# GpSimd's large operations in the recurrent layers: one a step, issued between VectorE's two products, and r projected before v

## The chip, the cores and the metric

One core of a Trainium2 chip runs the whole program. The metric is the device time of one execution in microseconds; smaller is better. Five engines work side by side, each in the order its instructions were issued: TensorE (PE in the profile, with PEld for its weight loads), VectorE (DVE), ScalarE (ACT), GpSimd (POOL) and SyncE (SP, which issues weight loads). Work on one engine waits for another through semaphores.

## The reference, cut to what matters

Four layers run one after the other on x (4 x 512 x 512, float32) and a context of the same shape: a cross attention (layer 0), two recurrent layers (1 and 2), and a perceiver attention with an MLP (layer 3). The change is in the recurrent layers. One of them computes, for a batch element and 512 time steps, with 32 heads of 16:

```
xa = layer_norm(x);  sx = previous_row(xa) - xa                 # "shift"
t  = tanh((xa + sx * maa_x) @ maa_w1)                            # first mix
m_j = t_j @ maa_w2_j;  x_j = xa + sx * (maa_j + m_j)             # j in w, k, v, r, g
w = exp(-exp(decay + tanh(xw @ dw1) @ dw2))
r, k, v = xr @ Wr, xk @ Wk, xv @ Wv;   g = silu(xg @ Wg)
for each step l:  a = k_l (x) v_l                                # outer product per head
    out_l = r_l . (faaaa * a + s);   s = a + w_l * s
y = group_norm(out) * gn_w + gn_b
x = x + (y * g) @ Wo
xc = layer_norm(x);  sxc = previous_row(xc) - xc                 # "shift" again
x = x + sigmoid((xc + sxc*fr) @ fWr) * (relu((xc + sxc*fk) @ fWk)**2 @ fWv)
```

The term faaaa * a needs only r*k summed over a head, times v: in the kernel ruk (faaaa * r * k), al (its sum by a matmul) and y = v * al.

## The kernel before, in words

`recurrent` cuts the two layers into 16 units (2 layers, 4 batch elements, 2 halves of TS = 256 rows), and each unit into G = 8 steps of the recurrence. A step g is: `begun(g+1)` multiplies the repeated v (in PSUM) with k (in SBUF) twice on VectorE, into kv and into A (line 833), copies the state into kv's first column (839), lets GpSimd add A onto kv by an accumulating DMA (`added`, 584), and has ScalarE copy the decay into W (844). `scan(g)` runs VectorE's scan over W and kv (866) and then two products with r, called ry (871). `summed(g-1)` sums an earlier step's ry on TensorE into py (885). A has one buffer, so the A product of a step waits until the DMA of the step before has landed. kv has two buffers.

Around the steps stand three generators for every unit: `mixes` (norm, shift, the five mixes, the projections), `outputs` (group norm, gate, Wo) and `channels` (the second half of the layer). Each yields a step and a phase (EARLY, SOON, MID, LATE) at which its next piece is issued. Steps count from the unit's own first step, so in any step pieces of several units meet: `mixes` of the next unit at -11 to 0, `outputs` of the last one at 9 to 15, `channels` of the one before it at 19 to 27. In the text "step 7" means any step with that place in a unit. The order inside a step is written out by hand: summed, begun, scan, the repetition of v (814) in every fourth, then the phases. The planner takes this order as it is; engines run ahead of one another only as far as buffers allow. PSUM has three rotating banks for all projections (`pp`), one for py and a single buffer for the repeated v.

GpSimd has six large operations a unit, each over 128 partitions: the shift of the mixes, sx (588, 128x1020, with a small second part for the first column, 589); ruk times k (772); v times al into y (799); the addition of rk onto half of y (800); y's gate, yg times g (958); and the shift of the channels, sxc (588, 589). In the kernel before they are issued in the phases, where their data come to be ready: sx at -9 MID, ruk at -2 EARLY, both y at 0 LATE, yg at 14 EARLY, sxc at 22 MID. Other work on GpSimd's queue: all accumulating DMAs (kv, mixes, xk, xr, x), and two small powers of 6.5 us for the group norm (933, 935).

ScalarE evacuates the projections: o_v, o_k, o_r (702) with two scalings ruk after each half of r (705), the gate o_g (698, finished by VectorE's `gated`, 717), the mixes (665), xk and xr from sxc (996), rp from the group norm's power (939), the gated output's scaling yg (951). The gate o_g has two buffers; one is read until yg's multiplication is over.

TensorE's order in the steps at which the change bites: step 7 is xa's transposes (ptn), Wo, then the next step's py; step 0 is al, the first mix (mixx with w1, two groups), xk's projection fk, and the first pair of mixes (w and k); step 1 is py, the mean, the second pair (v and r) and xr's projection pr; step 2 is py, the repetition vr, var; step 4 is v's projection, step 5 pbc and r's, step 6 py, vr, transposes, g's.

Of the kernel before, what the change touches and what calls it, by code (L numbers as in the profile page):

```python
# [8 lines left out]
F32 = mybir.dt.float32  # L9
I32 = mybir.dt.int32  # L10
AF = mybir.ActivationFunctionType
ALU = mybir.AluOpType
# [3 lines left out]
P = 128  # L16
# [5 lines left out]
BUFS = {"mix": 4, "cx": 3}  # L22
# [8 lines left out]
def tile_xattn_rwkv_perceiver(ctx: ExitStack, tc: tile.TileContext, t: dict, out: bass.AP):  # L31
    nc = tc.nc
# [422 lines left out]
    def recurrent(lp, ep, beside):  # L455
# [4 lines left out]
        G = 2 * NI  # L460
        TP = TS // 2
        EARLY, SOON, MID, LATE = range(4)

        mp = sp = mq = sq = pvr = pyp = W = A = None
# [19 lines left out]
        gmean = lp.tile([P, P], F32, name="gmean")  # L484
        nc.vector.tensor_scalar(gmean, gself, 1.0 / HS, None, ALU.mult)

        rp = lp.tile([P, TS], F32, name="rp")
        nc.gpsimd.memset(rp, 0.0)
        stT = lp.tile([P, KC, B, 2], F32, name="stT")
# [50 lines left out]
        def seconds(a):  # L540
            return a[:, :, TP:]
# [44 lines left out]
        def shift(sx, cur, before):  # L586

            nc.gpsimd.tensor_tensor(sx[:, :, 1:], cur[:, :, : TS - 1], cur[:, :, 1:], ALU.subtract)
            nc.gpsimd.tensor_tensor(sx[:, :, 0], before, cur[:, :, 0], ALU.subtract)

        st = {}

        def mixes(q):

# [20 lines left out]
            else:  # L615
                both = wpool.tile([P, 2, KC, TS], F32, tag="w", name="sx0")
                sx, mix = both[:, 0], both[:, 1]
            shift(sx, cur, stT[:, :, b, 1] if hf == 0 else st[q - 1]["last"])
            yield (-10, EARLY) if q == 1 else (-9, LATE)
            if mp:  # L620
                mix = mp.tile([P, KC, TS], F32, tag="mix", name="mixx", bufs=BUFS["mix"])
            for k in range(KC):
                nc.vector.scalar_tensor_tensor(
                    mix[:, k], sx[:, k], vec[:, k, V_MAAX : V_MAAX + 1], cur[:, k], ALU.mult, ALU.add
                )
            yield (-10, MID) if q == 1 else (-8, EARLY)
            th = lp.tile([P, 2, TS], F32, tag="th", name="th")
            pm = psum_tile([P, TS], "pm")
            mm(pm, [(c["w1"][:, k, :P], mix[:, k, :]) for k in range(KC)])
# [86 lines left out]
                for dst, pm in gates:  # L716
                    nc.vector.scalar_tensor_tensor(dst, dst, 1.0, pm, ALU.add, ALU.mult)

            yield (-7, EARLY) if q == 1 else (-8, LATE)
            second("wk")  # L720
            yield -7, MID if q == 1 else EARLY
            second("vr")
            yield -7, LATE
            mixed("wk")
# [28 lines left out]
            yield -5, LATE  # L753
            second("g")
            yield -4, MID
            if q > 0:
                product("v")
            else:
                ruk = mp.tile(full, F32, tag="mix", name="ruk", bufs=BUFS["mix"])
                product("r")  # L760
            yield -4, LATE
            mixed("g")
            yield -3, MID
            if q > 0:
                ruk = mp.tile(full, F32, tag="mix", name="ruk", bufs=BUFS["mix"])
                product("r")
            else:
                product("v")
                repeated(0, 0)
            yield -2, EARLY  # L770
            k, r = d["k"], d["r"]
            nc.gpsimd.tensor_tensor(ruk, ruk, k, ALU.mult)
            rk = mp.tile([P, NI, TP], F32, tag="rk", name="rk", bufs=1)
            nc.vector.tensor_tensor(rk, seconds(r), firsts(k), ALU.mult)
            D = d["D"] = mp.tile([P, NI, TP], F32, tag="D", name="D", bufs=1)
# [20 lines left out]
            )  # L796
            yield 0, LATE
            y = d["y"] = mq.tile(full, F32, tag="y", name="y")
            nc.gpsimd.tensor_tensor(y, d["v"], al[:, None, :].to_broadcast(full), ALU.mult)
            nc.gpsimd.tensor_tensor(seconds(y), seconds(y), rk, ALU.add)  # L800
            if q == 0:
                product("g")
                yield 1, LATE
# [21 lines left out]
        def begun(g):  # L825

            q, e, i = place(g)
            d = st[q]
            if units[q][2]:
                d["S"] = st[q - 1]["S"]  # L830
            kv = kvs[g] = mp.tile([P, 8, TP + 1], F32, tag="kv", name="kv")
            for half, dst in ((seconds, kv), (firsts, A)):
                nc.vector.tensor_tensor(
                    dst[:, :, 1:],
                    half(vrs[q, e].rearrange("p q f l -> p (q f) l")),
                    half(d["k"][:, i : i + 1, :]).to_broadcast([P, 8, TP]),
                    ALU.mult,
                )
            nc.vector.tensor_copy(quarters(kv)[:, :, :, 0], states(q)[:, i, e])  # L839
            if g == 0:  # L840
                nc.vector.tensor_tensor(flat(kv), flat(kv), flat(A), ALU.add)
            else:
                added(flat(kv), flat(A))
            nc.scalar.copy(W[g % 2][:, :, 1:], d["D"][:, i : i + 1, :].to_broadcast([P, 8, TP]))
# [5 lines left out]
        def quarters(kv):  # L850
            return kv.rearrange("p (q f) l -> p q f l", f=2)

        def states(q):
            return st[q]["S"].rearrange("p i (q e f) -> p i e q f", e=2, f=2)
# [45 lines left out]
        def outputs(q):  # L900
# [41 lines left out]
            mm(pm, [(gself, rp)])  # L942
            bc = sq.tile([P, TS], F32, tag="mean", name="bc", bufs=1)
            nc.scalar.copy(bc, pm)
            yield 13, LATE
            nc.vector.tensor_tensor(y, y, bc[:, None, :].to_broadcast(full), ALU.mult)
            yield 14, EARLY

            yg = mq.tile(full, F32, tag="cx", name="yg", bufs=BUFS["cx"])
            for i in range(NI):  # L950
# [4 lines left out]
                    bias=c["gn"][:, i, 1:2],  # L955
                    scale=c["gn"][:, i, 0:1],
                )
            nc.gpsimd.tensor_tensor(yg, yg, d["g"], ALU.mult)
            yield 15, MID
            wo = wpool.tile([P, NI, C], F32, tag="w", name=n + "wo")  # L960
            for a in range(4):
# [13 lines left out]
        def channels(q):  # L975
# [12 lines left out]
            nc.scalar.copy(last, cur[:, :, TS - 1])  # L988
            yield 22, MID
            sx = mq.tile([P, KC, TS], F32, tag="sxc", name="sxc", bufs=1)  # L990
            shift(sx, cur, stT[:, :, b, 0] if hf == 0 else st[q - 1]["lastc"])

            def shifted(name, i):
                dst = mq.tile([P, KC, TS], F32, tag="cx", name=name, bufs=BUFS["cx"])
# [2 lines left out]
                added(dst, cur)  # L997
                return dst

            yield 23, EARLY  # L1000
            xk = shifted("xk", V_FK)
            yield 23, LATE
            xr = shifted("xr", V_FR)
# [59 lines left out]
        with ExitStack() as below, ExitStack() as above:  # L1063
            mq = below.enter_context(tc.tile_pool(name="rq", bufs=2))
            sq = below.enter_context(tc.tile_pool(name="rt2", bufs=2))
            pp = below.enter_context(tc.tile_pool(name="rpp", bufs=3, space=PSUM))
            mp = above.enter_context(tc.tile_pool(name="rm", bufs=2))
            sp = above.enter_context(tc.tile_pool(name="rs", bufs=2))
            pvr = above.enter_context(tc.tile_pool(name="rpv", bufs=1, space=PSUM))
            pyp = above.enter_context(tc.tile_pool(name="rpy", bufs=1, space=PSUM))  # L1070
            psum["p"] = pp, "p"


            W = [mp.tile([P, 8, TP + 1], F32, tag=f"W{i}", name=f"W{i}", bufs=1) for i in range(2)]
            A = mp.tile([P, 8, TP + 1], F32, tag="A", name="A", bufs=1)
            for z in (*W, A):
                nc.gpsimd.memset(z[:, :, 0:1], 0.0)
            for g in range(at[0], end + 28):
                if 0 < g <= end:
                    summed(g - 1)  # L1080
                if -1 <= g < end - 1:
                    begun(g + 1)
                if 0 <= g < end:
                    scan(g)
                if 0 < g < end - 2 and g % NI == NI - 2:
                    repeated(*place(g + 2)[:2])
                for ph in (EARLY, SOON, MID, LATE):
                    for q, gen in steps.pop((g, ph), ()):
                        at = next(gen, None)
                        if at:  # L1090
                            follow(q, at, gen)
                    if ph == MID and 0 < g <= end and g % NI == 0:
                        taken(g - 1)
                if g == end:
                    above.close()
                elif g > end:
                    next(beside, None)
            for _ in beside:
                pass
# [409 lines left out]
```

## Time and profile before

| what | value |
|---|---|
| median of 3 runs | 3722.05 us (3721.71 to 3724.03) |
| span of the profiled execution | 3715.9 us |
| the profiled execution's own time | not given apart from its span; the runs lie 5.8 to 8.1 us above it |
| TensorE, VectorE, ScalarE, GpSimd busy | 95%, 73%, 45%, 47% of the span |
| recurrent steps (first scan to the end of the last py) | about 781 to 2254 us |
| layer 3 alone | from about 2410 us |
| ry (871) | 256 of 1598 ns in the mean, 398.6 us |
| scan (866) | 128 of 2311 ns, 295.9 us |

A row of a group or timeline gives the line, the engine, the operation, the output and its inputs by the program's names, the shape, how often, and the busy time; in brackets stand the engine's idle time before it and what ended it. A busy TensorE is not TensorE at its peak, since ends of pipelined matmuls are modelled. In a table of windows the columns are the length, the busy time (and number) for PE, PEld, DVE, ACT and POOL, the granted TensorE clock, the share of the DMA engines and GB/s.

### The profile page before, as it was taken

The numbers are of one execution on the slowest core, as the hardware profiler recorded it, in microseconds if no ns is written. First come the engines' busy times: TensorE is split into PE (matmuls) and PEld (weight loads), VectorE is DVE, ScalarE is ACT, GpSimd is POOL, SyncE is SP. The second block draws the span as 40 slices with busy tenths as digits, with TensorE's granted clock in tenths as the row PEclk, the third lists the DMA queues.
The fourth block names the chain that finished last, engine by engine and source line by source line (L and its number), as shares of the span: only waits on it lengthen the run. The fifth ranks groups of instructions, "written<-read, shape, count | busy, mean of one in ns | idle before, by whom it ended". The sixth has DMA issues, their size and how long they took to land. (4 is left out here: it accounts for less than half of the span.)

```text
span 3715.9 us, 52436 instructions
## 1 busy us (share of the span) xinstructions
PE 3545.8 (95%) x20544; PEld 1885.9 (51%) x20544; DVE 2728.7 (73%) x4601; ACT 1675.7 (45%) x2550; POOL 1743.4 (47%) x850
## 2 busy tenths in 40 slices
PE   8999999998899999999999988999999999999989
PEld 3333333365566665666666644444455444544446
DVE  6777777679988888888888883388855676667531
ACT  4777676544444444444444433233344334434421
POOL 4777777524444444444444443065533343444430
PEclk9999999999999999999999998999999999999999
DMA  4000000056677777777777775300022212121223
GB/s 154 24 12 24 12 9 21 24 130 140 146 177 175 177 187 182 176 175 177 177 175 177 177 167 134 102 26 18 23 88 77 72 52 88 60 71 35 97 97 125
DMA packets 188806, 386.67 MB, mean 104 GB/s; under 512 B 18128, under 2 KB 44880, under 8 KB 186512
## 3 DMA queue, kind: packets, MB, share of 16 engines
q1 hardware_dynamic: 150256, 251.72, 21.2%
q0 software_dynamic: 38304, 131.61, 19.4%
q8 instruction: 162, 2.65, 0.3%
q14 instruction: 84, 0.69, 0.1%
HBM read 247.50 MB, written 4.19 MB: 68 GB/s over the span
## 5 line engine op out<-in xcount | busy, mean ns | idle before, releaser
L1253 POOL TENSOR_TENSOR acc<-acc,aT 128x2048 f32<-128x2048 f32 x96 | 436.2, 4544 | 336.2 <-ACT aT L1248 219.6
L292 POOL TENSOR_TENSOR aT<-aT,nmT 128x1536 f32<-128x1536 f32 x124 | 428.6, 3460 | 206.1 <-ACT aT L290 182.8
L254 DVE CUSTOM_DVE_ANT_0 sc<-psc,nm 128x512 f32<-128x512 f32 x512 | 353.8, 691 | 146.8 <-PE psc L242 89.1
L1237 DVE TENSOR_TENSOR aT<-pst,mb 128x512 f32<-128x512 f32 x512 | 317.5, 681 | 163.2 <-PE pst L1192 163.2
L871 DVE TENSOR_TENSOR ry<-kv,o_r 128x1024 f32<-128x1024 f32 x256 | 398.6, 1598 | 7.2 <-PE pm L73 0.5
L866 DVE TENSOR_TENSOR_SCAN kv<-W,kv 128x1032 f32<-128x1032 f32 x128 | 295.9, 2311 | 0.0
L584 POOL DMA_DIRECT2D kv<-A x127 | 111.4, 877 | 358.0 <-DVE kv L839 220.0
L290 ACT COPY aT<-pst 128x512 f32<-128x512 f32 x372 | 196.5, 594 | 177.2 <-PE pst L279 176.8
L298 ACT ACTIVATE aT<-aT 128x2048 f32<-128x2048 f32 x128 | 246.7, 1929 | 5.5 <-POOL aT L292 4.8
L73 PE MATMUL ph<-nT,l_m 128*128 128x256 f32 x1024 | 235.9, 385 | 0.0
L73 PE MATMUL po<-l_m,hT 128*128 128x512 f32 x512 | 233.1, 601 | 0.0
L73 PEld LDWEIGHTS ph<-nT,l_m 128*128 128x128 f32 x1024 | 191.8, 191 | 64.2 <-issue 24.8
L1206 DVE CUSTOM_DVE_ANT_0 sc<-psc,zeros,mx 128x512 f32<-128x512 f32 x256 | 176.6, 745 | 56.2 <-PE psc L1192 47.1
L279 PE MATMUL pst<-q,km 32*128 32x512 f32 x1024 | 206.3, 639 | 9.4 <-DVE mxs L254 5.8
L1248 ACT ACTIVATE aT<-aT 128x2048 f32<-128x2048 f32 x64 | 122.3, 1910 | 190.6 <-DVE aT L1237 185.7
L1246 ACT ACTIVATE aT<-aT,mc 128x2048 f32<-128x2048 f32 x64 | 128.1, 2002 | 162.6 <-DVE aT L1237 156.3
L1206 DVE CUSTOM_DVE_ANT_0 sc<-psc,nm 128x512 f32<-128x512 f32 x256 | 161.1, 684 | 52.2 <-PE psc L1192 52.2
L242 PE MATMUL psc<-km,q 32*128 32x512 f32 x1024 | 197.8, 650 | 0.8 <-ACT q L223 0.8
L885 PE MATMUL py<-ry,k 128*32 128x512 f32 x1024 | 161.9, 625 | 38.3 <-DVE ry L871 25.6
L1192 PE MATMUL pst<-q,kT 32*128 32x512 f32 x1024 | 183.1, 649 | 0.0
L1192 PE MATMUL psc<-kT,q 32*128 32x512 f32 x1024 | 171.0, 644 | 12.3 <-DVE aT L1237 11.5
L1251 POOL TENSOR_TENSOR acc<-aT 128x2048 f32<-128x2048 f32 x16 | 72.5, 4532 | 234.2 <-ACT aT L1246 234.2
(266 smaller groups left out, 6999.6 us busy)
## 6 DMA issues: line engine op xcount, KB each, us to landing
l_m<-in_L_W SPq DMA_DIRECT2D x64, 1024.0 KB, 5.1
kv<-A POOLq DMA_DIRECT2D x127, 516.0 KB, 6.1
L_wk<-in_L_Wk SPq DMA_DIRECT2D x16, 1024.0 KB, 8.0
L_wr<-in_L_Wr SPq DMA_DIRECT2D x16, 1024.0 KB, 7.2
L_wv<-in_L_Wv SPq DMA_DIRECT2D x16, 1024.0 KB, 5.8
L_wg<-in_L_Wg SPq DMA_DIRECT2D x16, 1024.0 KB, 7.6
L_wo<-in_L_Wo SPq DMA_DIRECT2D x64, 256.0 KB, 4.9
L_fk<-in_L_fWk SPq DMA_DIRECT2D x16, 1024.0 KB, 6.8
```

The lines of the kernel that those rows point to most:

```text
L73: nc.tensor.matmul(ps, lhsT, rhs, start=(i == 0), stop=(i == len(pairs) - 1))
L242: nc.tensor.matmul(psc, d["q"][g][rs, lt * P : (lt + 1) * P], d["km"][rs, a, :], start=True, stop=True, tile_position=(32 * r, 0),)
L254: nc.vector.tensor_tensor_reduce(sc, ps[r], d["nm"][lt], 1.0, -3.0e38, ALU.add, ALU.max, mxs[:, a, lt, c : c + 1])
L279: nc.tensor.matmul(pst, d["km"][rs, a, s * P : (s + 1) * P], d["q2", a][rs, :], start=True, stop=True, tile_position=(32 * r, 0),)
L292: nc.gpsimd.tensor_tensor(w[:, n:, :], w[:, n:, :], nmT[:, None, :].to_broadcast([P, NR - n, L]), ALU.add)
L298: nc.scalar.activation(w, w, AF.Exp)
L866: nc.vector.tensor_tensor_scan(flat(kv), flat(W[g % 2]), flat(kv), 0.0, ALU.mult, ALU.add)
L871: nc.vector.tensor_tensor(y, kv[:, 4 * h : 4 * h + 4, None, :TP].to_broadcast([P, 4, 2, TP]), d["r"][:, i].rearrange("p (o m) -> p o m", o ...
L1192: nc.tensor.matmul(psc, lhsT[rs], rhs[rs], start=True, stop=True, tile_position=(32 * r, 0))
L1206: nc.vector.tensor_tensor_reduce(sc, ps[r], d["nm"][a], 1.0, mx[:, 0, lt, r : r + 1] if a else 3.0e38, ALU.add, ALU.min, mx[:, a, lt, r : ...
L1237: nc.vector.tensor_tensor(w[:, r, :], ps[r], d["mb"][:, r, :], ALU.subtract)
L1253: nc.gpsimd.tensor_tensor(d["acc", m], d["acc", m], w, ALU.add)
```

## The change

A helper `pooled` collects the six large operations in `slots`, by step. `begun` issues those of the current step after the kv and A products have been issued, behind a GpSimd copy of one element of kv to a tile `mark`; the copy makes GpSimd wait for the kv product, not for A. The operations are set to steps -8 (sx), -3 (ruk), 1 and 2 (y), 14 (yg) and 23 (sxc), one in any step. kv's DMA is issued on GpSimd's queue after them. For the first two units the steps below 0 are issued at once. The copy of the state moves ahead of the products. r is projected before v in every unit. The first mix moves from -9 LATE and -8 EARLY to -8 EARLY and -8 LATE, behind fk; the pairs of mixes from -8 LATE and -7 EARLY to -7 EARLY and -7 MID; y times bc from 13 LATE to 13 MID, yg's scaling from 14 EARLY to 13 LATE, and xk from 23 EARLY to 23 SOON.

```diff
--- before.py
+++ after.py
@@ -484,6 +484,7 @@
         gmean = lp.tile([P, P], F32, name="gmean")
         nc.vector.tensor_scalar(gmean, gself, 1.0 / HS, None, ALU.mult)
 
+        mark = lp.tile([P, 1], F32, name="mark")
         rp = lp.tile([P, TS], F32, name="rp")
         nc.gpsimd.memset(rp, 0.0)
         stT = lp.tile([P, KC, B, 2], F32, name="stT")
@@ -589,6 +590,14 @@
             nc.gpsimd.tensor_tensor(sx[:, :, 0], before, cur[:, :, 0], ALU.subtract)
 
         st = {}
+        slots = {}
+
+        def pooled(q, at, f, *args):
+
+            if q < 2 and at < 0:
+                f(*args)
+            else:
+                slots.setdefault(G * q + at, []).append(lambda: f(*args))
 
         def mixes(q):
 
@@ -615,15 +624,15 @@
             else:
                 both = wpool.tile([P, 2, KC, TS], F32, tag="w", name="sx0")
                 sx, mix = both[:, 0], both[:, 1]
-            shift(sx, cur, stT[:, :, b, 1] if hf == 0 else st[q - 1]["last"])
-            yield (-10, EARLY) if q == 1 else (-9, LATE)
+            pooled(q, -8, shift, sx, cur, stT[:, :, b, 1] if hf == 0 else st[q - 1]["last"])
+            yield (-10, EARLY) if q == 1 else (-8, EARLY)
             if mp:
                 mix = mp.tile([P, KC, TS], F32, tag="mix", name="mixx", bufs=BUFS["mix"])
             for k in range(KC):
                 nc.vector.scalar_tensor_tensor(
                     mix[:, k], sx[:, k], vec[:, k, V_MAAX : V_MAAX + 1], cur[:, k], ALU.mult, ALU.add
                 )
-            yield (-10, MID) if q == 1 else (-8, EARLY)
+            yield (-10, MID) if q == 1 else (-8, LATE)
             th = lp.tile([P, 2, TS], F32, tag="th", name="th")
             pm = psum_tile([P, TS], "pm")
             mm(pm, [(c["w1"][:, k, :P], mix[:, k, :]) for k in range(KC)])
@@ -716,9 +725,9 @@
                 for dst, pm in gates:
                     nc.vector.scalar_tensor_tensor(dst, dst, 1.0, pm, ALU.add, ALU.mult)
 
-            yield (-7, EARLY) if q == 1 else (-8, LATE)
+            yield -7, EARLY
             second("wk")
-            yield -7, MID if q == 1 else EARLY
+            yield -7, MID
             second("vr")
             yield -7, LATE
             mixed("wk")
@@ -753,23 +762,17 @@
             yield -5, LATE
             second("g")
             yield -4, MID
-            if q > 0:
-                product("v")
-            else:
-                ruk = mp.tile(full, F32, tag="mix", name="ruk", bufs=BUFS["mix"])
-                product("r")
+            ruk = mp.tile(full, F32, tag="mix", name="ruk", bufs=BUFS["mix"])
+            product("r")
+            k, r = d["k"], d["r"]
+            pooled(q, -3, nc.gpsimd.tensor_tensor, ruk, ruk, k, ALU.mult)
             yield -4, LATE
             mixed("g")
             yield -3, MID
-            if q > 0:
-                ruk = mp.tile(full, F32, tag="mix", name="ruk", bufs=BUFS["mix"])
-                product("r")
-            else:
-                product("v")
+            product("v")
+            if q == 0:
                 repeated(0, 0)
             yield -2, EARLY
-            k, r = d["k"], d["r"]
-            nc.gpsimd.tensor_tensor(ruk, ruk, k, ALU.mult)
             rk = mp.tile([P, NI, TP], F32, tag="rk", name="rk", bufs=1)
             nc.vector.tensor_tensor(rk, seconds(r), firsts(k), ALU.mult)
             D = d["D"] = mp.tile([P, NI, TP], F32, tag="D", name="D", bufs=1)
@@ -796,8 +799,8 @@
             )
             yield 0, LATE
             y = d["y"] = mq.tile(full, F32, tag="y", name="y")
-            nc.gpsimd.tensor_tensor(y, d["v"], al[:, None, :].to_broadcast(full), ALU.mult)
-            nc.gpsimd.tensor_tensor(seconds(y), seconds(y), rk, ALU.add)
+            pooled(q, 1, nc.gpsimd.tensor_tensor, y, d["v"], al[:, None, :].to_broadcast(full), ALU.mult)
+            pooled(q, 2, nc.gpsimd.tensor_tensor, seconds(y), seconds(y), rk, ALU.add)
             if q == 0:
                 product("g")
                 yield 1, LATE
@@ -829,6 +832,7 @@
             if units[q][2]:
                 d["S"] = st[q - 1]["S"]
             kv = kvs[g] = mp.tile([P, 8, TP + 1], F32, tag="kv", name="kv")
+            nc.vector.tensor_copy(quarters(kv)[:, :, :, 0], states(q)[:, i, e])
             for half, dst in ((seconds, kv), (firsts, A)):
                 nc.vector.tensor_tensor(
                     dst[:, :, 1:],
@@ -836,7 +840,11 @@
                     half(d["k"][:, i : i + 1, :]).to_broadcast([P, 8, TP]),
                     ALU.mult,
                 )
-            nc.vector.tensor_copy(quarters(kv)[:, :, :, 0], states(q)[:, i, e])
+            large = slots.pop(g - 1, ())
+            if large:
+                nc.gpsimd.tensor_copy(mark, kv[:, 0, 1:2])
+            for f in large:
+                f()
             if g == 0:
                 nc.vector.tensor_tensor(flat(kv), flat(kv), flat(A), ALU.add)
             else:
@@ -942,9 +950,9 @@
             mm(pm, [(gself, rp)])
             bc = sq.tile([P, TS], F32, tag="mean", name="bc", bufs=1)
             nc.scalar.copy(bc, pm)
+            yield 13, MID
+            nc.vector.tensor_tensor(y, y, bc[:, None, :].to_broadcast(full), ALU.mult)
             yield 13, LATE
-            nc.vector.tensor_tensor(y, y, bc[:, None, :].to_broadcast(full), ALU.mult)
-            yield 14, EARLY
 
             yg = mq.tile(full, F32, tag="cx", name="yg", bufs=BUFS["cx"])
             for i in range(NI):
@@ -955,7 +963,7 @@
                     bias=c["gn"][:, i, 1:2],
                     scale=c["gn"][:, i, 0:1],
                 )
-            nc.gpsimd.tensor_tensor(yg, yg, d["g"], ALU.mult)
+            pooled(q, 14, nc.gpsimd.tensor_tensor, yg, yg, d["g"], ALU.mult)
             yield 15, MID
             wo = wpool.tile([P, NI, C], F32, tag="w", name=n + "wo")
             for a in range(4):
@@ -988,7 +996,7 @@
             nc.scalar.copy(last, cur[:, :, TS - 1])
             yield 22, MID
             sx = mq.tile([P, KC, TS], F32, tag="sxc", name="sxc", bufs=1)
-            shift(sx, cur, stT[:, :, b, 0] if hf == 0 else st[q - 1]["lastc"])
+            pooled(q, 23, shift, sx, cur, stT[:, :, b, 0] if hf == 0 else st[q - 1]["lastc"])
 
             def shifted(name, i):
                 dst = mq.tile([P, KC, TS], F32, tag="cx", name=name, bufs=BUFS["cx"])
@@ -997,7 +1005,7 @@
                 added(dst, cur)
                 return dst
 
-            yield 23, EARLY
+            yield 23, SOON
             xk = shifted("xk", V_FK)
             yield 23, LATE
             xr = shifted("xr", V_FR)
@@ -1080,6 +1088,8 @@
                     summed(g - 1)
                 if -1 <= g < end - 1:
                     begun(g + 1)
+                for f in slots.pop(g, ()):
+                    f()
                 if 0 <= g < end:
                     scan(g)
                 if 0 < g < end - 2 and g % NI == NI - 2:
```

## The prediction

> **What bounds the kernel now.** I read the page first, then stretches of the span with each engine's busy time, then TensorE's waits in one unit, and last the timelines around the six operations. The page:
>
> ```profile
> PE 3545.8 (95%) x20544; PEld 1885.9 (51%) x20544; DVE 2728.7 (73%) x4601; ACT 1675.7 (45%) x2550; POOL 1743.4 (47%) x850
> L871 DVE TENSOR_TENSOR ry<-kv,o_r 128x1024 f32<-128x1024 f32 x256 | 398.6, 1598 | 7.2 <-PE pm L73 0.5
> ```
>
> TensorE is busy 95%. VectorE's two ry products a step take 1598 ns in the mean, though undisturbed ones take 1209 to 1224: something lengthens some of them. The recurrent layers run from 781 to 2254 us. Busy times of the second unit and of a middle one (columns: length, PE, PEld, DVE, ACT, POOL, clock, DMA):
>
> ```profile
> 864.70:949.50 84.80, 75.50 (x573) 49.44 (x572) 81.47 (x79) 34.57 (x68) 40.61 (x23) 0.98 0.65 144
> 1420.70:1516.10 95.40, 91.58 (x627) 58.26 (x627) 83.11 (x87) 44.13 (x88) 44.23 (x31) 1.00 0.77 178
> ```
>
> Two regimes. In units 0 to 2 VectorE is nearly full (81 of 85) and TensorE waits. In units 3 to 13 (eleven, each about 95.4 from scan to scan) TensorE is full: its waits in this middle unit are six, 3.7 us in all:
>
> ```profile
> PE py L885 <- DVE ry L871: 0.8, 1, 0.8
> PE pbc L73 <- ACT rp L939: 0.7, 1, 0.7
> PE ptn L572 <- DVE o_g L717: 0.6, 1, 0.6
> PE pmm L654 <- ACT mix_w L665: 0.6, 1, 0.6
> PE var L921 <- ACT y L916: 0.5, 1, 0.5
> PE pmm L654 <- ACT mix_v L665: 0.5, 1, 0.5
> ```
>
> Only ry and o_g are VectorE's. So in eleven units of sixteen the change is worth what it does to TensorE's waits; VectorE idles 12 us there. [...]
>
> **How the six operations now collide.** A lengthened ry always lies beside a GpSimd operation. The place nearest to what the change makes is the end of unit 15, where sxc already runs beside a scan (first the timeline of POOL, then of DVE):
>
> ```profile
> 2240.84 2.86 POOL L588 TENSOR_TENSOR sxc<-xc 128x1020 f32<-128x1020 f32 x1
> 2243.66 2.20 POOL L589 TENSOR_TENSOR sxc<-lastc,xc 128x4 f32<-128x4 f32 x1
> 2247.90 0.88 POOL L584 DMA_DIRECT2D xk<-xc  x1 [2.04 <-ACT xk L996]
> ```
> ```profile
> 2241.88 3.98 DVE L866 TENSOR_TENSOR_SCAN kv<-W,kv 128x1032 f32<-128x1032 f32 x1
> ```
>
> The scan (alone 2.29) ends at 2245.86 instead of 2244.2: it waited for sxc. And the tiny second part of the shift, 128x4, alone 0.21 (1501.87), took 2.20 and ended with the scan at 2245.86: it waited for VectorE in turn. The two engines alternate, instruction by instruction.
>
> **The change part by part.** *Start beside the PSUM products.* With k0 the start of VectorE's kv product: the product ends at k0+1.21, POOL reacts 0.30 later (1420.82 to 1421.12), the mark copy is bounded by 0 and the 0.21 of the 128x4 row (I take 0.2): the operation starts at k0+1.7. Beside PSUM products it runs at its own length (sxc 1.89 beside o_g's; yg 2.39 with VectorE idle). The A product is over at k0+2.3, so the scan waits until k0+3.6 for sxc and k0+4.0 for the multiplications. VectorE loses 1.3 to 1.7 where ry lost 2.0 to 2.2. A gain, but half of what the words promise, since the scan has two SBUF inputs like ry. Over a unit I count sxc 1.3, sx 1.3, y 1.5, yg 2 (it waits for ScalarE's yg and meets ry), ruk 0 (VectorE idles then): 6.1 at most against 6.3 of today (1.99, 2.19 and 2.15 on three ry), and about 5.3 in all likelihood, since A waits for kv's DMA at step 0 while sx runs.
>
> *TensorE's gains in a full unit, at step 7* (times from G, the end of g's projection, 1499.43):
>
> ```profile
> 1500.22 0.66 PE L572 MATMUL ptn<-ident,z 128*128 128x128 f32 x4
> 1501.47 0.66 PE L572 MATMUL ptn<-ident,z 128*128 128x128 f32 x4 [0.60 <-DVE o_g L717]
> 1510.02 2.19 PE L885 MATMUL py<-ry,k 128*32 128x512 f32 x8 [0.79 <-DVE ry L871]
> ```
>
> o_g is late because POOL's yg (1497.68, 2.39) holds the gate's buffer until 1500.1. In the change ScalarE's yg follows v's copy directly, a step phase earlier, and yg ends about 4 us earlier by my count: the 0.60 goes. The gates then end at about k0 = G+1.45 instead of G+2.5. ry ends at k0+3.6+2.30+2.36 = G+9.7 (today 1511.09, G+11.7), and py 1.1 later as today: G+10.8 instead of 1512.21, G+12.8. **Gain 1.9** (TensorE alone would allow 2.6; the least, 0.6).
>
> *What is late next: xk.* Today sxc is done at 1502.1, ScalarE scales xk, the DMA is issued at 1506.09 and lands 6.3 later (6.3 to 6.6 in all full units, 4.5 to 4.9 in the drain), at G+13.0. TensorE needs it at 1518.52 (G+19.1): al, then mixx's 3.7 us, then fk. The change issues sxc a step later, and puts fk directly behind al. New chain: sxc ends k0+3.6, the scan takes 2.3, sxc's second part ends with it at k0+5.9, the DMA follows 2.04 later as at 2247.90: G+9.4. kv's DMA, held behind both parts, goes just ahead. L_wk's 1 MB is issued at the same moment (today 1509.25); xr, issued beside it, takes 9.0 from its true issue at 1510.8, while xk today is clear of it. Landing between 4.5 and 9.0; I take 7.0, nearer to today's xk: G+16.4. al ends at G+10.8+2.7 = G+13.5. **A new wait of 2.9**, bounds 0.4 and 4.9. Queued behind fk are mixx, py and everything of the unit; nothing covers it.
>
> *r ahead of v.* r's evacuation puts two ruk scalings ahead of rp on ScalarE:
>
> ```profile
> 1479.57 0.59 ACT L702 COPY o_v<-pm 128x512 f32<-128x512 f32 x1 [2.81 <-PE pm L689]
> 1480.05 1.00 ACT L939 COPY rp<-gn_rs 32x64 f32<-32x64 f32 x4
> 1489.79 0.85 ACT L705 ACTIVATE ruk<-pm,L_u 128x256 f32<-128x256 f32 x2
> ```
>
> pbc already waits 0.7 for rp, so **+0.8** (bounds 0 and 0.85). The lengths 7.09 and 7.63 of the projections only trade places. ruk, at step 5 in POOL's queue ahead of kv's DMA, waits for ScalarE until about 1481.6; kv's DMA then goes at 1484.1 instead of 1477.2 and lands 5.4 to 6.3 later, where A and then vr of step 6 need it: **+0.2** on TensorE (bounds 0 and 1.5). y's product with bc moves ahead of the statistics and makes VectorE wait about 4 us for bc; VectorE idles there anyway.
>
> *The mixes later.* The second pair (vr) now stands behind pr at the end of step 1; ScalarE's mix_r ends 1.2 after TensorE's last (1440.71 against 1439.52), then W and the square, 2.0 together (1447.12 to 1449.11). TensorE's py and vr cover 2.1 of these 3.2. var waits 1.1 instead of 0.5: **+0.6** (bounds 0 and 1.2). Weight loads on SP only swap L_wr and L_wv: nothing, since each is issued 20 us ahead; without that cover one costs up to 8 us.
>
> Sum per full unit: -1.9 + 2.9 + 0.8 + 0.2 + 0.6 = +2.6; eleven units, +29. Units 0 to 2, bound by VectorE: lengthening of 5.5, 7.8 and 9.7, of which I give back 1 each, -3; there kv's DMA behind sx's second part (k0+6, landing 4.6 to 6.2 later, A due about k0+11.4) takes up to 0.8 back. Units 14 and 15 and the drain: 0, between -3 and +4 (the shift moves one step later there, beside layer 3's work). Together +26. The profile's span is 3715.9; the page gives no other time of that execution, and the runs (3721.71 to 3724.03) lie about 6.1 above it. 3715.9 + 26 + 6.1 = 3748.
>
> **The rivals.** *Faster: xk is in time and the ScalarE waits stay covered.* For it: xk has 6 us of slack today; if sxc's second part slipped in before the scan, xk would come 2.3 earlier. Against it: the row at 2243.66. It decides at step 7 when xk lands before G+13.5. Gains alone, 11 x 2.6 + 3 = 32: 3690. [...]
>
> *Same.* xk in time, rp, vr and var as worked out: (-1.9 + 1.6) x 11 - 3 = -6: 3716.
>
> *Slower still.* xk queues like xr (9.0, or 11.2 from its first issue): a wait of 4.9 to 7.1, +22 to +46 on the forecast: 3770 to 3794. For it: mix_v, issued beside L_wr, takes 9.1. Against it: xk's bytes stand behind kv's alone in their own queue.
>
> **How the numbers follow.** Forecast 0.50, slower still 0.18, same 0.12, faster 0.20. 0.2% is 7.4 us, about what a measurement tells from no change. The range 3700 to 3785 leaves out half of the faster case and half of the much slower one; the forecast alone has 3728 to 3770.
>
> **What would show it.** Right: in a full unit fk waits for xk's DMA 0.4 to 5 us, pbc waits about 1.5 for rp, o_g's wait is gone, py is near 1.1 long, scans beside POOL are 1.3 to 1.7 longer and most ry 1.2. Wrong: if sxc's second part stays near 0.2, if fk shows no wait, or if units 3 to 13 come out under 95.4.

## The result, and the profile after

The changed kernel takes **3801.93 us** (median of four runs, 3800.06 to 3803.22) against 3721.88 (3718.61 to 3724.03) for the kernel before: a ratio of 1.0217, 95% interval 1.0203 to 1.0232. The forecast was 3748 with a range up to 3785. The sign was right; the size was short by 54 us, and the range did not hold it.

The page of the profiled execution after (its span is 3800.0 us, against 3715.9):

```profile
PE 3564.8 (94%) x20544; PEld 1908.0 (50%) x20544; DVE 2706.3 (71%) x4601; ACT 1676.1 (44%) x2550; POOL 1779.9 (47%) x938
L879 DVE TENSOR_TENSOR ry<-kv,o_r 128x1024 f32<-128x1024 f32 x256 | 342.1, 1378 | 6.9
L874 DVE TENSOR_TENSOR_SCAN kv<-W,kv 128x1032 f32<-128x1032 f32 x128 | 327.8, 2561 | 0.7 <-ACT xk L1004 0.7
L73 PE MATMUL pm<-xk,L_fk 128*128 128x256 f32 x512 | 139.2, 439 | 86.3 <-DVE mixx L632 55.3
```

What the words of the change promise is there: ry's mean falls from 1598 to 1378 ns, VectorE is busy 22 us less, and the scan takes part of the lengthening over. The bill is in the fourth line: fk's 512 matmuls stand behind 86.3 us of idle time. ("DVE mixx" cannot be what it waited for: mixx is not an operand of fk. The transfer of xk is: three of the eleven full units name it for the same wait, and the next views show it.)

The spans differ by 84.1 us and the medians by 80.1, because the execution profiled before was about 4 us quicker than its median (the times on record lie 1.7 to 2.1 us above their spans). Where the 84.1 us lie, from the first scan of each unit to the first scan of the next:

| stretch | before | after | difference |
|---|---|---|---|
| up to unit 0 | 780.6 | 783.4 | +2.8 |
| units 0 to 2 | 256.9 | 254.6 | -2.3 |
| units 3 to 13 | 1052.7 | 1126.9 | +74.2 |
| unit 14 | 90.5 | 103.4 | +12.9 |
| unit 15, seven steps | 61.2 | 65.1 | +3.9 |
| the rest | 1474.1 | 1466.5 | -7.6 |

A full unit takes 102.4 us instead of 95.4. First TensorE's waits in one full unit after (1448.1 to 1550.4), then its timeline at the seam of two units (start, length, group, and in brackets the idle time before the group):

```profile
PE pm L73 <- DVE mixx L632: 6.1, 1, 6.1
PE pbc L73 <- ACT rp L947: 1.3, 1, 1.3
PE var L929 <- ACT y L924: 1.1, 1, 1.1
PE pmm L663 <- ACT mix_w L674: 0.5, 1, 0.5
```
```profile
1443.87 1.67 PE L893 MATMUL py<-ry,k 128*32 128x512 f32 x8
1445.47 2.00 PE L73 MATMUL al<-ruk,ksel 128*128 128x256 f32 x8
1447.30 1.05 PE L73 MATMUL al<-rk,ksel 128*128 128x128 f32 x8
1454.43 9.02 PE L73 MATMUL pm<-xk,L_fk 128*128 128x256 f32 x32 [6.07 <-DVE mixx L632]
```

The waits for o_g (0.6) and ry (0.8) are gone, as forecast. In their place fk waits 6.1, and then its product itself takes 9.02 instead of 7.17. The reason for the second is in the clock (columns: length, busy time of PE, PEld, DVE, ACT, POOL with instructions, granted clock, DMA share, GB/s):

```profile
1445.00:1449.00 4.00, 3.36 (x20) 2.49 (x16) 3.90 (x6) 1.79 (x4) 2.95 (x4) 1.00 0.94 215
1449.00:1454.40 5.40, 0.00 (x0) 0.01 (x1) 5.37 (x6) 0.00 (x0) 2.89 (x2) 0.72 1.04 212
1454.40:1458.00 3.60, 3.57 (x9) 2.89 (x10) 3.07 (x6) 0.00 (x0) 0.46 (x2) 0.50 1.05 209
1458.00:1463.30 5.30, 5.30 (x26) 4.69 (x25) 4.03 (x3) 1.23 (x2) 2.89 (x2) 0.98 0.27 53
```

While TensorE waits, its clock falls to 0.50 and stays there until 1458.2; fk's first matmuls run at half speed (up to 766 ns each, where the product's median is 380). The same rows suggest why xk is late: the DMA engines are full (share 0.94 to 1.05) until it has landed. First GpSimd's timeline, then the scan on VectorE, then the issues of 1436 to 1465 with their median time to landing:

```profile
1437.99 1.88 POOL L589 TENSOR_TENSOR sxc<-xc 128x1020 f32<-128x1020 f32 x1
1439.84 2.20 POOL L590 TENSOR_TENSOR sxc<-stT,xc 128x4 f32<-128x4 f32 x1
1441.98 0.87 POOL L585 DMA_DIRECT2D kv<-A  x1
1444.08 0.85 POOL L585 DMA_DIRECT2D xk<-xc  x1 [1.23 <-PE pm L73]
```
```profile
1438.83 3.21 DVE L874 TENSOR_TENSOR_SCAN kv<-W,kv 128x1032 f32<-128x1032 f32 x1
```
```profile
L_wk<-in_L_Wk SPq DMA_DIRECT2D x1, 1024.0 KB, 7.8
...
xk<-xc POOLq DMA_DIRECT2D x1, 512.0 KB, 10.1
xr<-xc POOLq DMA_DIRECT2D x1, 512.0 KB, 11.0
```

sxc's tiny second part takes 2.20 and ends with the scan at 1442.04, as forecast. ScalarE then scales xk, which is issued at 1444.08; SP's load of L_wk was issued at 1443.97, when wo's last matmul released its buffer. xk lands at 1454.18, 10.1 us after its issue, where it took 6.3 to 6.6 before.

### The profile page after: what moved, and what is told of

The parts are those of the page before. It is cut to its first block, busy times and chain, and to the rows that moved or that the text cites. A ratio compares the mean times of both kernels' runs of the same rounds, so it can differ in the third digit from the quotient of the medians.

```text
span 3800.0 us, 52545 instructions
## 1 busy us (share of the span) xinstructions
PE 3564.8 (94%) x20544; PEld 1908.0 (50%) x20544; DVE 2706.3 (71%) x4601; ACT 1676.1 (44%) x2550; POOL 1779.9 (47%) x938
## 4 chain that ended last, share of the span: by engine, by line
PE 61%; DVE 7%; DMA 3%; ACT 3%; issue 2%; POOL 2%; POOLq 0%; DVEq 0%; ACTq 0%
PE pm L73 11%; PE ph L73 6%; PE pv L73 6%; PE po L73 6%; PE pm L698 5%; PE pst L1202 4%; PE psc L1202 4%; PE po L1268 3%; PE pk L73 3%; PE pr L73 3%; PE pmm L663 2%; DMA kv<-A 2%; DVE kv L874 2%; PE py L893 1%; DVE ry L879 1%
## 5 line engine op out<-in xcount | busy, mean ns | idle before, releaser
L879 DVE TENSOR_TENSOR ry<-kv,o_r 128x1024 f32<-128x1024 f32 x256 | 342.1, 1378 | 6.9
L874 DVE TENSOR_TENSOR_SCAN kv<-W,kv 128x1032 f32<-128x1032 f32 x128 | 327.8, 2561 | 0.7 <-ACT xk L1004 0.7
L73 PE MATMUL pm<-xk,L_fk 128*128 128x256 f32 x512 | 139.2, 439 | 86.3 <-DVE mixx L632 55.3
L837 DVE TENSOR_TENSOR A<-vr,o_k 128x1024 f32<-128x1024 f32 x128 | 156.0, 1218 | 40.4 <-DMA kv<-A 39.5
L1202 PE MATMUL psc<-kT,q 32*128 32x512 f32 x1024 | 171.5, 644 | 12.3 <-DVE aT L1247 11.5
```

What stands on the lines that cost most here:

```text
L73: nc.tensor.matmul(ps, lhsT, rhs, start=(i == 0), stop=(i == len(pairs) - 1))
L874: nc.vector.tensor_tensor_scan(flat(kv), flat(W[g % 2]), flat(kv), 0.0, ALU.mult, ALU.add)
L879: nc.vector.tensor_tensor(y, kv[:, 4 * h : 4 * h + 4, None, :TP].to_broadcast([P, 4, 2, TP]), d["r"][:, i].rearrange("p (o m) -> p o m", o ...
L1202: nc.tensor.matmul(psc, lhsT[rs], rhs[rs], start=True, stop=True, tile_position=(32 * r, 0))
```

## The experiments

The theory after the result: the loss is one chain, sxc late, xk issued beside L_wk's load, fk waiting 6 us, the clock halved behind the wait. The rivals: the order of r and v, the late mixes, or VectorE. Each difference is to the kernel before unless another is named.

**sxc put back, alone.**

```
-            pooled(q, 23, shift, sx, cur, ...)
+            shift(sx, cur, ...)
...
-            yield 23, SOON
+            yield 23, EARLY
```

> The kernel after, with channel mixing's shift (sxc) alone put back to where it was issued before (directly at step 22, phase MID, with xk's scaling at step 23, EARLY); fk still follows al directly. Theory: the loss sits in the chain from sxc to fk's product, the wait of 6.1 us per full unit and the 1.85 us that fk's matmuls then run longer at half clock. With xk scaled about 6 us earlier it lands before al ends; fk's wait falls below 0.5, fk's product takes 7.2 again, a full unit takes about 94.5 instead of 102.4, and the time comes to 3700 to 3720. Rival one: the loss comes from the order of r and v and the late mixes on ScalarE: a full unit stays above 99 and the time above 3770. Rival two: xk's DMA is slow because of what lies beside it, not because of its issue: fk still waits 3 us or more, and the time is 3750 or more.

Measured: 3714.33 us, ratio 0.9981 (0.9972 to 0.9991). A full unit takes 94.6 or 96.3 us. xk is issued 3.8 us ahead of L_wk's load, lands 6.6 after its issue, and fk follows al with no wait (TensorE's timeline of this kernel):

```profile
1417.69 1.05 PE L73 MATMUL al<-rk,ksel 128*128 128x128 f32 x8
1418.58 6.64 PE L73 MATMUL pm<-xk,L_fk 128*128 128x256 f32 x30
```

One operation of six carries the whole loss, 88 us. With the other five moved, the change is a small gain.

The wait for o_g is back in this kernel, with 0.6 us, although yg ends as early as after the change. sxc now follows yg directly and lies beside VectorE's two ry, which take 6.28 us where they took 4.57 after the change, and the gates o_g stand behind these on VectorE:

```profile
1397.84 6.28 DVE L879 TENSOR_TENSOR ry<-kv,o_r 128x1024 f32<-128x1024 f32 x2
```

**sxc moved, alone, in the kernel before.** The only edits to the kernel before are the small copy, the slot for sxc and the later yield for xk.

> The kernel before, with sxc alone moved (begun behind a small copy that follows VectorE's kv product, one step later; xk's scaling at step 23, SOON); the other five operations, the mixes and the orders of the projections stay. mixx's 3.7 us of matmuls still stand between al and fk. Theory: xk is issued 5 to 6 us later than before and lands 6 to 10 us after its issue, while TensorE needs it 3.7 us later than in the kernel after and py has not become earlier: a wait of 0 to 2 us per full unit, almost no time at half clock, 3722 to 3750. Rival: the move of sxc costs the whole loss by itself, wherever fk stands: a wait of about 6 and 3780 or more. Other rival: no wait at all and ry shorter in one step: 3705 to 3722.

Measured: 3764.89 us, ratio 1.0115 (1.0100 to 1.0130): above the theory's 3750, below the rival's 3780. Here mixx's 3.7 us lie between al and fk, and xk takes 10.1 us again, beside L_wk issued at 1426.22 (TensorE):

```profile
1432.43 1.91 PE L639 MATMUL pm<-mixx,L_w 128*32 128x256 f32 x8
1436.72 8.83 PE L73 MATMUL pm<-xk,L_fk 128*128 128x256 f32 x32 [2.38 <-issue]
```

The wait is 2.4, a little over what was expected. That the clock would fall behind so short a wait was not: fk takes 8.83 instead of 7.17 (mean granted clock of the execution 0.969, against 0.977 before). A full unit takes 98.2, or 100.0 where the clock falls a second time. So the late sxc loses with fk behind mixx too, though less: 43 us.

**TensorE kept busy while fk waits.** The added matmuls read operands of al and write columns that nobody reads.

```
+            if 2 <= q:
+                mm(pm[:, TS + TP :], [(kself, rk[:, i % NI, :]) for i in range(24)])
```

> The kernel after, with 24 added matmuls of 128 columns on TensorE between al and fk in units 2 to 15 (into columns of al's PSUM tile that nobody reads), so that TensorE does not idle while fk waits for xk. Theory: fk's product takes 9.0 instead of 7.2 because the clock falls to half after 6 us of idling; with the idle time filled down to 1 us or less, the granted clock stays near 1 at fk's start, fk's product takes 7.2 to 7.5, and the time falls by 1.5 to 1.9 us in each of 12 units: 3777 to 3786. Rival: fk's product is long because its weights or xk come in late, or because of what runs beside it: it stays at 9.0 and the time is within 5 us of 3802, or above it by what the added matmuls take.

Measured: 3786.32 us, ratio 1.0172 (1.0157 to 1.0187), 15.6 less than after. Useless work made the kernel faster. TensorE in one unit:

```profile
1649.83 3.51 PE L73 MATMUL al<-rk,ksel 128*128 128x128 f32 x30
1654.04 7.14 PE L73 MATMUL pm<-xk,L_fk 128*128 128x256 f32 x32 [0.69 <-DMA xk<-xc]
```

fk takes 7.14 at a granted clock of 1.00: the 1.85 were the clock's. The undisturbed full units take 100.4 to 100.8. In five of the eleven a drop of 3.4 us comes at another place, and four of these five take 102.2 to 103.3; in two more xk takes 11.5 us to land and TensorE still waits 2.1 ahead of fk. That is why the time ends at the upper edge of what was expected.

**L_wk's load held back.** An added matmul inside fk's product reads L_wo, so that L_wo's buffer, which L_wk takes, comes free in the middle of fk.

```
+                if m and 1 <= q < len(units) - 1:
+                    held = st[q + 1]["wo"]
+                    mm(pm[:, 0, :P], [(held[:, 0, :P], held[:, 0, :P])])
```

> The kernel after, in which one added matmul of 128 columns inside fk's product (before its second half) still reads the weights L_wo, so that L_wk's load of 1 MB, which takes L_wo's buffer, is issued some 12 to 15 us later than now, behind xk's and xr's transfers. Theory: xk's DMA takes 10.1 us instead of 6.3 because L_wk's load, issued 0.1 us ahead of it, shares the DMA engines with it. Without it xk lands 6 to 7.5 us after its issue, fk's wait falls from 6.1 to 2.5 to 3.5 us, one stretch of half clock instead of two follows, a full unit takes 98.5 to 100, and the time comes to 3755 to 3780. Rival: xk's 10.1 us come from kv's and xr's transfers in its own queue: it still lands 9 us or more after its issue and the time stays within 8 us of 3802.

Measured: 3726.73 us, ratio 1.0016 (1.0007 to 1.0026): 75 us less than after, far more than expected. The issues of 1415 to 1450 and TensorE at the seam:

```profile
L_wk<-in_L_Wk SPq DMA_DIRECT2D x1, 1024.0 KB, 8.0
...
xk<-xc POOLq DMA_DIRECT2D x1, 512.0 KB, 5.2
xr<-xc POOLq DMA_DIRECT2D x1, 512.0 KB, 6.0
```
```profile
1425.61 1.05 PE L73 MATMUL al<-rk,ksel 128*128 128x128 f32 x8
1427.78 3.69 PE L73 MATMUL pm<-xk,L_fk 128*128 128x256 f32 x16 [1.12 <-DMA xk<-xc]
```

xk lands in 5.2 us instead of 10.1, with sxc as late as ever and kv's and xr's transfers still beside it. The wait is 1.1, the clock stays at full speed in all but one of the units concerned (mean granted clock of the execution 0.976, against 0.965 after), and a unit takes 95.8 (102.3 in unit 3, which the edit leaves alone). The load that started 0.1 us ahead of xk makes 6.6 of the 7.0 us that a full unit lost: 5.0 of wait and the rest of clock.

**v ahead of r again**, with ruk's product issued directly as before, the rest as after.

```
+            if q > 0:
+                product("v")
...
+                product("r")
...
+            nc.gpsimd.tensor_tensor(ruk, ruk, k, ALU.mult)
```

> The kernel after, with the projections of r and v in the order of before (v at step -4, r at step -3, ruk's product on GpSimd issued directly at step -2). Theory: two scalings of r on ScalarE, 0.85 each, no longer stand ahead of rp; TensorE's wait for rp falls from 1.28 to about 0.74, a full unit takes 0.5 to 0.8 less, 3793 to 3797. If r's order costs nothing because fk waits for xk's DMA anyway: within 3 us of 3802. If v's evacuation or yg is later by it and o_g's wait comes back, the gain is lost: 3800 to 3812.

Measured: 3823.16 us, ratio 1.0272 (1.0247 to 1.0297), 21 more than after. TensorE's waits in a full unit:

```profile
PE pm L73 <- DVE mixx L632: 6.0, 1, 6.0
PE var L935 <- ACT y L930: 1.1, 1, 1.1
PE ptn L573 <- DVE o_g L726: 1.0, 1, 1.0
PE pbc L73 <- ACT rp L953: 0.7, 1, 0.7
```

rp's wait falls to 0.7, and o_g's comes back with 1.0: units 4 to 8 take 102.2 to 102.8, as after. So the gain is lost, as the last case of the expectation has it, though the time lies above that too: the rest is in units 9 to 14 (105.0 to 105.9), where the trace has 10.2 to 13.7 us of half clock a unit instead of 6.8.

**Fewer operations moved.** Three kernels leave some of the six where they were before. The first puts back sxc, sx and the mixes; the second also r behind v and ruk; the third is the kernel before with yg alone:

```
-            yield 13, LATE
+            yield 13, MID
             nc.vector.tensor_tensor(y, y, bc[:, None, :].to_broadcast(full), ALU.mult)
-            yield 14, EARLY
+            yield 13, LATE
...
-            nc.gpsimd.tensor_tensor(yg, yg, d["g"], ALU.mult)
+            pooled(q, 14, nc.gpsimd.tensor_tensor, yg, yg, d["g"], ALU.mult)
```

> The kernel after, with sxc and also time mixing's shift (sx), the mixes and w1's products put back to where they were before; y's two operations, ruk and yg still begin beside VectorE's products, and r still goes ahead of v. Against the kernel with sxc alone put back (3714, with var's wait 1.1 and rp's 1.3, and in 7 of 12 units 1.7 us of half clock behind the two waits for the mixes). Theory: the late second pair of mixes is what makes var wait 0.6 more: that goes, and a full unit takes 94.0 where the clock stays up: 3695 to 3710. Rival: time mixing's shift beside the scan is itself worth its 0.5 to 1.3 us a unit: 3715 to 3725.

> As the one before, and the projections of v and r in the order of before, with ruk's product issued directly: of the six operations only y's two and yg still begin beside VectorE's products. Theory: rp's wait falls from 1.28 to 0.74, and o_g's wait stays at 0.6 or grows to 1.0: against the one before between -0.54 and -0.1 a unit, 3690 to 3708. Rival: yg comes later with v's earlier or later evacuation, o_g waits for more than 1 us, and the time is 3710 or more.

> The kernel before with one part of the change alone: y's product with the group norm's factors half a step earlier, ScalarE's yg behind it, and GpSimd's product with the gate begun behind VectorE's kv product. Theory: this part carries the whole gain at step 7; VectorE's ry there is no longer lengthened and TensorE's py waits for nothing: 1.9 us less in each of eleven units, o_g's wait of 0.6 unchanged: 3698 to 3708. Rival: the gain needs y's operations moved too, or the clock falls to half behind a new pattern of waits in many units: 3712 or more.

Measured: 3727.57 (ratio 1.0012, 1.0002 to 1.0022), 3752.01 (1.0075, 1.0060 to 1.0090) and 3751.70 us (1.0078, 1.0063 to 1.0093). All three theories fell. In the first, sx beside ry at step 7 costs most of what it cost before (TensorE):

```profile
1420.01 2.19 PE L893 MATMUL py<-ry,k 128*32 128x512 f32 x8 [0.51 <-DVE ry L879]
```

py is 2.19 long behind a wait of 0.5 (0.3 in every second unit), where with sx moved it took 1.06 without a wait. So the move of sx is worth 13 us (3714 against 3727), more than its late mixes cost. In the third, yg alone, o_g's wait is 2.3 in the unit shown and 2.8 in most. GpSimd's timeline there, then VectorE's:

```profile
1405.57 2.39 POOL L597 TENSOR_TENSOR yg<-yg,o_g 128x1024 f32<-128x1024 f32 x1 [4.36 <-ACT yg L962]
1407.91 0.90 POOL L585 DMA_DIRECT2D kv<-A  x1
1408.57 2.72 POOL L778 TENSOR_TENSOR ruk<-ruk,o_k 128x1024 f32<-128x1024 f32 x1
1411.25 2.34 POOL L589 TENSOR_TENSOR sxc<-xc 128x1020 f32<-128x1020 f32 x1
```
```profile
1408.97 2.87 DVE L780 TENSOR_TENSOR rk<-o_r,o_k 128x512 f32<-128x512 f32 x1
1411.76 2.37 DVE L782 TENSOR_TENSOR D<-o_w 128x512 f32<-128x512 f32 x1
```

yg waits 4.4 us for ScalarE at the head of GpSimd's queue. Behind it ruk and sxc come to lie beside VectorE's rk and D, which take 2.87 and 2.37 instead of 0.68, and the gates o_g stand behind those. With r ahead of v, ruk is done a step earlier: the first of these kernels has r ahead and waits 0.6 for o_g, the second differs from it in this order and ruk's place alone and waits 2.8 in most units. So it is the order of r and v, with ruk's place, that makes yg's move affordable.

**rp's copies earlier, and towards a faster kernel.** In the changed kernel rp's four copies stand behind r's evacuations on ScalarE; GpSimd's second power ends about 3 us before the first of these. The edit is `yield 12, LATE` to `yield 12, SOON` ahead of the copies: on the kernel with sxc put back, on the one with L_wk held back (there in all units), and on the kernel before.

> The kernel after with sxc alone put back (3714), and rp's four small copies issued half a step earlier on ScalarE, ahead of r's evacuations and ruk's scalings instead of behind them. Theory: the 1.29 us that TensorE's pbc waits for rp come only from that order: GpSimd's second power ends about 3 us before r's first evacuation, so the copies fit into ScalarE's idle time, the wait goes, and a full unit takes 1.2 to 1.4 us less: 3694 to 3704. Rival: another wait behind it (bc, yg, o_g's gate) takes its place: 3708 or more.

> The kernel after with L_wk's load held back as before, now in the first full unit too (102.3 there against 95.8), and rp's copies early as in the run beside. All six operations still begin beside VectorE's products. Theory: 6.5 from the one unit and 1.3 from each of twelve: 3700 to 3712, so that the change with its two side effects removed is no slower than before, about 0.3 to 0.6% faster. Rival: xk's remaining wait of 1.1 grows by what is gained ahead of it, or the clock falls behind it again in most units: 3716 or more.

> The kernel before with rp's four copies alone issued half a step earlier. It tells what of the two runs above has nothing to do with the change. Theory: pbc's wait of 0.74 goes in eleven units: 3711 to 3716. Rival: the copies then wait on ScalarE ahead of v's evacuations, or the wait only moves to o_g: within 4 us of 3722.

Measured: **3698.83 us, ratio 0.9939 (0.9926 to 0.9951)**; 3717.93 (0.9986, 0.9977 to 0.9995); 3720.81 (0.9997, 0.9988 to 1.0005). The first beats both kernels, by 23 and 103 us. TensorE's waits in one of its full units (93.5 us):

```profile
PE var L929 <- ACT y L924: 1.1, 1, 1.1
PE ptn L573 <- DVE o_g L726: 0.5, 1, 0.5
PE pmm L663 <- ACT mix_w L674: 0.5, 1, 0.5
PE pmm L663 <- ACT mix_v L674: 0.5, 1, 0.5
```

rp's line is gone. With L_wk held back the same edit gains only 0.4 to 0.9 a unit (94.9 to 95.4 instead of 95.8, where the clock stays up), since vr then waits up to 0.9 for A, that is for kv's transfer. The rival's time came, but not for its reasons: xk's wait stayed at 1.1, and the clock fell in four of twelve units only. In the kernel before, the wait of 0.7 goes too (94.6 instead of 95.4), but in six of eleven units a drop of the clock (96.2 to 96.3) takes it back; before, there were two such units.

**The second pair of mixes directly behind the first**, on the fastest kernel (`yield -7, MID` to `yield -7, SOON`).

> As the kernel with sxc put back and rp early, and the second pair of mixes directly behind the first, ahead of fr's product instead of behind it. Theory: ScalarE's statistics chain is no longer behind the late pair, var's wait falls from 1.07 to 0.5, and the two waits of 0.5 for the mixes fall into one stretch; the drop to half clock behind fr's product in 7 of 12 units goes or moves: between 3 and 15 us below the run without it, 3683 to 3700. Rival: the second pair waits longer for the first one's evacuation (1 to 2 us) than var gains: within 3 us of the run without it, or slower.

Measured: 3728.91 us, ratio 1.0018 (1.0009 to 1.0027), 30 slower than without the edit. TensorE waits less, and yet a unit takes 96 to 98. Its timeline, then stretches of the same time:

```profile
1150.82 1.56 PE L663 MATMUL pmm<-th,L_w 32*128 32x256 f32 x10
1152.87 1.42 PE L663 MATMUL pmm<-th,L_w 32*128 32x256 f32 x8 [0.50 <-ACT mix_w L674]
1154.51 3.96 PE L663 MATMUL pmm<-th,L_w 32*128 32x256 f32 x14 [0.22 <-ACT mix_w L674]
1158.40 7.01 PE L73 MATMUL pr<-L_fr,xr 128*128 128x512 f32 x12
```
```profile
1151.40:1154.80 3.40, 2.68 (x18) 1.77 (x16) 3.40 (x4) 2.75 (x8) 0.00 (x0) 1.00 0.52 97
1154.80:1158.20 3.40, 3.40 (x14) 2.00 (x12) 3.40 (x5) 2.68 (x9) 0.99 (x2) 0.50 0.00 0
1158.20:1161.60 3.40, 3.40 (x5) 1.51 (x5) 3.40 (x3) 1.15 (x3) 3.02 (x4) 0.50 0.93 173
```

With waits of 0.5 and 0.2 us only, the clock is at 0.50 for 6.8 us, in every full unit (10.2 in three of them). The expectation allowed for a slower kernel, but through longer waits.

## Why the prediction was wrong

**Right.** A full unit is TensorE's, and VectorE's saving buys nothing by itself: VectorE is busy 22 us less and the kernel is 80 slower, while the fastest kernel above, 23 faster, has VectorE as busy as before (2727.9 against 2728.7). The gain of 1.9 was there (o_g's 0.60, and a wait and a py of 2.98 together that became a py of 1.67). But the reason given for o_g's part, yg ending earlier, was half of it: with sxc put back yg still ends early and o_g waits 0.6, so that sxc's move was needed too. The new wait is at the place named, of fk for xk. xk's issue was worked out at G+9.4, counted from the end of g's projection, and came at G+8.9; al's end at G+13.5 came at G+13.2. rp cost 0.54 (0.8 taken, bounds 0 and 0.85), var 0.56 (0.6 taken); the 0.2 for kv's DMA did not appear. Units 0 to 2 gave 2.3 (3 taken).

**The step that failed: "Landing between 4.5 and 9.0; I take 7.0, nearer to today's xk".** It took 10.1, outside the bounds: the wait was 6.1, not 2.9, and its upper bound of 4.9 was too low. The working named L_wk's load as issued at the same moment, and then took the row of a transfer that was clear of it. The nearer row was the other one, xr's 9.0 to 11.2, which runs beside that load. Without the load the same transfer landed in 5.2, and the wait was 1.1: most of the wait hung on this one neighbour. The second rival ("slower still", xk queues like xr) had the mechanism and its wait (4.9 to 7.1), with 0.18 of chance; the measured 3802 lies above its 3770 to 3794. "Faster" and "same" both needed xk in time; where it was, with sxc put back, the time was 3714, close to the 3716 of "same". That closeness is partly chance: this kernel has o_g's wait again and 3.4 us of half clock in seven of twelve units, and neither is in that sum.

**Left out: what a wait does behind itself.** No term had the clock. With the wait of 6.1 it falls to 0.50 for 6.8 us (until 1458.2 in the unit shown), and fk's product takes 1.85 longer in each unit; refilling the wait took that back (7.14 at a clock of 1.00). The rival's price is short by this term. So is the forecast's: with sxc moved alone, fk took 1.66 longer behind a wait of only 2.4, where the forecast had one of 2.9.

**Mis-sized: units 14 and 15 and what follows**, "0, between -3 and +4". They cost 12.9 and 3.9, and 7.6 came back later. With L_wk held back unit 14 takes 95.8, so the collision is 7.6 of its 12.9. Of the rest, step 5 grew from 10.5 to 14.3 us, where VectorE waits 3.9 for bc: "VectorE idles there anyway" is true of the full units and not of this one. That reading rests on the step lengths alone; no run tested it.

**Wrong in size, without effect on the sum.** The scan was expected 1.3 to 1.7 longer; it is 0.9 longer at step 7 and 0.4 to 0.7 elsewhere. The swap of r and v was priced as a cost alone (0.8 and 0.2); that it also keeps ruk clear of rk and D, as yg alone (3752) shows, was not seen.

The sum, then: -1.9 + 6.1 + 1.85 + 0.54 + 0.56 and 0.25 for r's product (7.88 instead of 7.63) is 7.4 a full unit, against 7.0 measured. Eleven units at 2.6 were 29; they were 74.2. These 45 and the 12 or 13 outside these units (9 at the end, the rest ahead of unit 3) make the miss of 58 in the span, which is 54 in the time.

## What to carry to other kernels

When a transfer is moved, list what is issued within a microsecond of its new place on every queue, and price it by a row that has that neighbour, not by its own old row (xk took 10.1 us beside L_wk's load and 5.2 without it). When a step creates a wait on TensorE, add what the clock does behind it (here 1.85 us behind a wait of 6.1), and judge an operation by the order of its whole queue: yg's move cost 30 us without r's, and sxc's was bad with the others and alone.

## What was not expected of the hardware

- The clock falls behind waits far shorter than the 6.1 us: behind one of 2.4 us with sxc moved alone (fk then 8.83 us instead of 7.17), and with the second pair of mixes moved behind a stretch with waits of 0.5 and 0.2 us only, where most matmuls were 32 rows deep (clock 0.50 for 6.8 us). In the clock records of the profiled executions before and after, between 1040 and 2180 us, the halved stretches last 3.41 us (two, before) or 6.83 us (twelve, after), and within one execution they start whole multiples of 3.41 us apart (860.2 us before, 102.4 us after). The same work in neighbouring units has a drop in some and none in others (96.3 and 94.6 us with sxc put back).
- How long TensorE is busy did not tell where a drop came. In the kernel before, it is busy for 2.91 us in each of four stretches of 3.41 us with the same work; behind two of them (from 1052.70 and 1912.86 us) the clock is 0.50, behind the two others (from 1721.68 and 1817.25 us) it is 1.00. The 128-row matmuls of pmean fill 0.4 to 0.5 us of the first two and 0.7 to 0.9 us of the others, and the remaining matmuls are 32 rows deep. No run varied the depth alone, so that the rows make the difference is not shown.
- One drop costs 1.7 us of a unit where TensorE is full (96.3 us instead of 94.6 with sxc put back), about what the edits here win or lose. A saved wait of 0.7 us in eleven units came to nothing that way (3720.81 us with rp's copies early in the kernel before, ratio 0.9997).
- With one 1 MB load (L_wk's) begun 0.1 us ahead of it on another queue, a 512 KB transfer (xk's) took 10.1 us; with that load held back it took 5.2.
